# The up-projections' blocks reordered once in memory, and a folding piece fetched by one load in place of 16

## The chip, the cores and the metric

The kernel runs on one core of a Trainium2 chip. The metric is the device time of one execution in microseconds (us); lower is better. The time before is 2107.13 us, the median of 3 runs (2104.47 to 2111.49). The core's engines are TensorE (PE in the profile; PEld is its weight load), VectorE (DVE), ScalarE (ACT), GpSimd (POOL) and SyncE (SP). SP does no arithmetic here: it issues DMAs, one after the other, and waits for what each needs before it issues it. A DMA's data is then moved by 16 DMA engines that all queues share.

## What is computed

Two layers, all in float32. Both normalise their input, add an attention branch and a feed-forward branch to it, and pass the sum on:

```
xn = layernorm(x);  x = x + attn0(xn) + ffn0(xn)
xn = layernorm(x);  x = x + attn1(xn) + ffn1(xn)
```

- `attn0`: a test-time-training scan. For 4 sequences of 512 tokens and 32 heads of width 16, in 32 steps of 16 tokens, a small weight matrix per head is updated by a gradient, and read by the queries.
- `ffn0`: `silu(gate) * up`, then `down`; width 512 to 1408 and back.
- `attn1`: latent attention, 16 heads of width 128. Keys and values come from a latent of 128 columns, queries from one of 384. The rotary part of a head (64 columns) is a further product with `W_QR` or `W_KR`:

```
c_kv = xn @ W_DKV + b_DKV;  k = c_kv @ W_UK;  v = c_kv @ W_UV
c_q  = xn @ W_DQ  + b_DQ;   q = c_q  @ W_UQ
q[..., :64] = rope(q @ W_QR);  k[..., :64] = rope(k @ W_KR)
probs = softmax(q k^T / sqrt(128));  out = (probs @ v) @ W_O + b_O
```

- `ffn1`: four experts, each a gated feed-forward of width 512.

`W_UK` is [128, 2048], `W_UQ` [384, 2048] and `W_UV` [128, 2048]; the 2048 columns are 16 heads of 128.

## The kernel before

The kernel is one function, `trunk_kernel`. Its order on each engine is set by a scheduler that builds the program: it moves independent instructions past each other, by its own estimate of when they are ready. Only instructions wrapped in `pin` or `fetch` (`keep_in_program_order`) keep the written order on their engine. The many small DMAs on SP are not pinned.

**Layer 0** (the trace's first 930 us or so). Tokens go in 8 chunks of 256 columns. A generator `between(ch)` (line 636) lists the work of a chunk beside the scan: 11 gate-up blocks `gate_up(ch, i)` (line 448), the normalisation and projections of the next chunk, and two `down` passes (line 464). Each piece yields its cost in us; the scan's loop (line 761) calls `fill(us)` in its gaps, which takes pieces from this list until their costs cover the gap. A gate-up block loads two weight tiles of 256 KB, `wg` and `wu` (line 454, two buffers of each), and makes 8 products of them (helper `mm`, line 100). A `down` pass loads 11 tiles `wd` of 256 KB (line 470, four buffers). A load can be issued as soon as TensorE is done with the buffer's last content. All of them, the rows of the scan's keys and values (`rows`, `kv`) and its results (`z`, line 437) go through SP's queue.

**The experts** (about 930 to 1175 us): `hidden` and `returned`, lines 940 to 974. The weights of the attention's first head group are folded beside them.

**Attention of layer 1** (about 1175 to 2107 us). The 16 heads go in 4 groups of 4. A unit is one head of one batch: 4 groups x 4 batches x 4 heads = 64 units, in the loop of line 1259. In unit i TensorE makes keys and queries (`pk`, line 1053; `pq`, line 1061) and scores (`sc`, line 1071), VectorE and ScalarE make the probabilities of unit i-1, VectorE turns them in blocks of 32 x 32 (`tt`, line 1100), and `turn` (line 1125) puts the blocks in their places by 16 DMAs of 64 KB on SP (line 1131). The context product of unit i-3 (`pc`, line 1139) reads them. Output products of a finished batch (`p`, `px`, line 1182) are spread over the units that follow. Once per batch the latents of the next one are loaded (`cq`, line 819, three DMAs).

**Folding** (`fold`, line 827). `W_QR` and `W_KR` are multiplied into the up-projections, and `W_UV` into `W_O`, one head group at a time, so that no unit pays for it. A group has five pieces: `W_UK`, the three row blocks of `W_UQ`, and `W_UV`, each 128 rows x 4 heads x 128 columns. The products need a piece transposed. VectorE transposes within blocks of 32 x 32 (`wt`, line 852), so the load must put the 4 x 4 blocks of each head into their transposed places: line 862 does this with 16 DMAs for each piece, one for each quarter of the columns (`dq`) and each head, of 16 KB in runs of 128 bytes. `raw` has two buffers in the attention stage. A step of the generator loads piece i, transposes piece i-2 and multiplies piece i-3 (`pw`, line 847). The loop advances it once in three of four units, from the second batch of the group before. The first 64 columns of each head go to `uk` and `uq` by a DMA each (line 832), and rows of `W_O` to `ow` (line 838, on GpSimd's queue in the attention stage).

Of the kernel before, what the change touches and what calls it, by code (L numbers as in the profile page):

```python
# [12 lines left out]
F32 = mybir.dt.float32  # L13
# [5 lines left out]
P = 128  # L19
# [25 lines left out]
H, D, KVC, QC, RD = 16, 128, 128, 384, 64  # L45
# [3 lines left out]
HPG = H // NHG  # L49
# [6 lines left out]
def trunk_kernel(ctx: ExitStack, tc: tile.TileContext, a: dict, out: bass.AP):  # L56
    nc = tc.nc
# [12 lines left out]
    dram = ctx.enter_context(tc.tile_pool(name="dram", bufs=1, space=bass.MemoryType.DRAM))  # L70
    yd = dram.tile([B, L, HS], F32, tag="yd", name="yd")
    xe_d = dram.tile([2 * NCHUNK, P, NC, E, 32], F32, tag="xe_d", name="xe_d")
    lat_d = dram.tile([1 + QC // P, P, B, NCHUNK, CT], F32, tag="lat_d", name="lat_d")
    bo = const.tile([P, HS], F32, tag="bo", name="bo")
    eps_ttt = const.tile([P, 1], F32, tag="eps_ttt", name="eps_ttt")
    nc.vector.memset(eps_ttt, TTT_EPS)

# [11 lines left out]
    with ExitStack() as px:  # L89
# [7 lines left out]
        quarters = [slice(32 * q, 32 * q + 32) for q in range(4)]  # L97

        def mm(out, lhsT, rhs, start=True, stop=True):
            nc.tensor.matmul(out, lhsT=lhsT, rhs=rhs, start=start, stop=stop, skip_group_check=True)  # L100

        def psum():
            return ps_pj.tile([P, 512], F32, tag="pj", name="pj")
# [48 lines left out]
        def by_head(name):  # L152

            return a[name].rearrange("(al r) (be bp h d) -> al r be bp h d", al=4, be=4, bp=2, h=2)[:, 0, :, 0]
# [4 lines left out]
        for name in ("gamma", "beta"):  # L159
            nc.scalar.dma_start(  # L160
                out=row[name].rearrange("o (be al x) -> o be al x", be=NC, al=4),
                in_=by_head(name).rearrange("al be h d -> be al (h d)").unsqueeze(0),
# [26 lines left out]
        for h in range(2):  # L189
            r = slice(4 * h, 4 * h + 4)  # L190
            nc.gpsimd.dma_start(
                out=sel8[r], in_=a["bones"].rearrange("(be h r) p -> h be r p", be=4, h=2)[h, :, 0]
# [4 lines left out]
        for al in range(4):  # L197
            for h in range(2):
                src = a["W1"].rearrange("p (be bp h d) -> p be bp h d", be=4, bp=2, h=2)
# [248 lines left out]
        def gate_up(ch, i):  # L448
            if i == 0:
                hid[ch] = wk.tile([P, NI, CW], F32, tag="hid", name=f"hid_{ch}", bufs=1)  # L450
            pf = ps_ff.tile([P, 2, CW], F32, tag="pf", name=f"pf_{ch}_{i}")
            for j, nm in enumerate(("wg", "wu")):
                w = wk.tile([P, NC, P], F32, tag=nm, name=f"{nm}_{ch}_{i}")
                nc.sync.dma_start(out=w, in_=a[nm][i])
                for c in range(NC):
                    mm(pf[:, j, :], w[:, c, :], xTs[ch][:, c, :], c == 0, c == NC - 1)
            sg = wk.tile([P, CW], F32, tag="sg", name=f"sg_{ch}_{i}")
            nc.scalar.activation(sg, pf[:, 0, :], AF.Silu, scale=gs[:, i : i + 1])  # L458
            nc.vector.scalar_tensor_tensor(  # L459
                hid[ch][:, i, :], pf[:, 1, :], us[:, i : i + 1], sg, ALU.mult, ALU.mult  # L460
            )
            yield 3.43
# [20 lines left out]
        for j, name in enumerate(("gamma", "beta")):  # L483
            nc.gpsimd.dma_start(
                out=ch8[4 * j : 4 * j + 4], in_=by_head(name).rearrange("al be h d -> be al (h d)")
# [150 lines left out]
        def between(ch):  # L636
# [4 lines left out]
            for i in range(NI):  # L641
                yield from gate_up(ch, i)
                if ch + 1 == NCHUNK and i in (2, 5, 8):
                    latent_rows(i // 3)
                if i == NI - 3:
                    yield from take(fin, 1)
# [162 lines left out]
    quarters = [slice(32 * q, 32 * q + 32) for q in range(4)]  # L809
# [4 lines left out]
    ups = ["uk"] + [f"uq{i}" for i in range(QC // P)]  # L814
# [11 lines left out]

    def fold(w, hg, wk, psum, bufs, pin=lambda ins: ins, ahead=1, rows=nc.sync):

        c = slice(hg * HPG * D, (hg + 1) * HPG * D)
        srcs = [a["W_UK"][:, c]] + [a["W_UQ"][i * P : (i + 1) * P, c] for i in range(QC // P)]  # L830
        for nm, src in zip(ups, srcs):
            nc.sync.dma_start(out=w[nm][:, :, :RD], in_=src.rearrange("p (h d) -> p h d", h=HPG)[:, :, :RD])
        srcs.append(a["W_UV"][:, c])
        raws, turned, ows = {}, {}, {}

        def output_rows(h):
            ows[h] = wk.tile([P, HS], F32, tag="ow", name=f"ow_{hg}_{h}", bufs=2)
            rows.dma_start(out=ows[h], in_=a["W_O"][(hg * HPG + h) * D : (hg * HPG + h + 1) * D, :])

        n = len(srcs)  # L840
        for i in range(n + 1 + ahead):
            k = i - ahead - 1
            if 0 <= k < n - 1:
                wt, wr, to = turned.pop(k), wqr if k else wkr, w[ups[k]]
                pw = psum(f"pw_{hg}_{i}").rearrange("p (h d) -> p h d", h=HPG)[:, :, :RD]
                for h in range(HPG):
                    pin(nc.tensor.matmul(pw[:, h, :], lhsT=wt[:, h, :], rhs=wr, start=True, stop=True))
                pin(nc.scalar.copy(to[:, :, RD:], pw))
            if 0 <= i - ahead < n:
                t = turned[i - ahead] = wk.tile([P, HPG, P], F32, tag="wt", name=f"wt_{hg}_{i - ahead}", bufs=1)  # L850
                pin(
                    nc.vector.transpose(
                        out=t.rearrange("p h c -> p (h c)"), in_=raws.pop(i - ahead).rearrange("p h c -> p (h c)")
                    )
                )
            if i < n:

                raw = raws[i] = wk.tile([P, HPG, P], F32, tag="raw", name=f"raw_{hg}_{i}", bufs=bufs)
                view = srcs[i].rearrange("(cq r) (h dq d) -> dq r h cq d", r=32, h=HPG, dq=4)
                for dq, r in enumerate(quarters):  # L860
                    for h in range(HPG):
                        nc.sync.dma_start(  # L862
                            out=raw[r, h].rearrange("r (cq d) -> r cq d", cq=4), in_=view[dq, :, h]
                        )
            if i - n - ahead + 1 >= 0:
                output_rows(i - n - ahead + 1)
            yield
        wt = turned.pop(n - 1)
        for h in range(HPG):
            pv = psum(f"pvo_{hg}_{h}")  # L870
            pin(nc.tensor.matmul(pv, lhsT=wt[:, h, :], rhs=ows[h], start=True, stop=True))
            pin(nc.scalar.copy(w["vo"][:, h, :], pv))
            hh = hg * HPG + h
            if hh == 0:
                pin(nc.vector.tensor_scalar_mul(bo_part, ows[h], buv[:, :1]))
            else:
                pin(nc.vector.scalar_tensor_tensor(bo_part, ows[h], buv[:, hh : hh + 1], bo_part, ALU.mult, ALU.add))
            if h + 2 < HPG:
                output_rows(h + 2)
            if h == 1:  # L880
                yield
        if hg == NHG - 1:
            pb = psum("pbo")
            pin(nc.tensor.matmul(pb, lhsT=ones, rhs=bo_part, start=True, stop=True))
            pin(nc.vector.tensor_add(bo, pb, bo))

    with ExitStack() as px:
# [88 lines left out]
        for e in range(E):  # L976
            if e == 1:
                nc.sync.dma_start(out=wqr, in_=a["W_QR"])
                nc.sync.dma_start(out=wkr, in_=a["W_KR"])
                buv16 = wk.tile([H, D], F32, tag="sg", name="buv16")  # L980
                nc.sync.dma_start(out=buv16, in_=a["b_UV"].rearrange("(h d) -> h d", d=D))
                w0 = group_tiles(lat, 0)
                cqs = {(0, 0): batch_latents(0, 0)}
                first = fold(w0, 0, wk, lambda nm: psp.tile([P, 512], F32, tag="pa", name=nm), 1)
                nc.sync.dma_start(out=buk, in_=a["b_UK"])
                nc.sync.dma_start(out=buq, in_=a["b_UQ"])
                for k in range(E):
                    nc.sync.dma_start(
                        out=trig_k[RD:, :].rearrange("p (k e j) -> p k e j", k=NCHUNK, e=E)[:, :, k],
                        in_=a["trig"][:, k * P : (k + 1) * P].rearrange("p (k j) -> p k j", k=NCHUNK),  # L990
                    )
                nc.sync.dma_start(out=ckv, in_=lat_d[0].rearrange("p b k x -> p b (k x)"))
# [28 lines left out]
    with ExitStack() as px:  # L1021
# [5 lines left out]
        def pin(ins):  # L1027
            tc.keep_in_program_order(ins)
            return ins
# [229 lines left out]
        for i in range(nu + 1):  # L1259
            if i < nu:  # L1260
                hg, b, h = units[i]
# [24 lines left out]
            if i >= 3:  # L1286
                hg, b, h = units[i - 3]
# [5 lines left out]
            k = i - (nu - HPG * B)  # L1293
# [113 lines left out]
```

## Time and profile before

| | |
|---|---|
| median of 3 runs | 2107.13 us |
| the profiled execution | 2108.69 us |
| its span, first to last instruction | 2106.9 us |
| mean granted TensorE clock | 0.982 of full speed |
| TensorE busy | 2004.7 us (95%) |
| VectorE, ScalarE, GpSimd busy | 1245.9, 843.3, 585.9 us |
| DMA share of SP's queue (q1) | 43.7% of 16 engines' span |
| DMAs of line 1131 | 1008, 0.60 us to issue (median) |
| DMAs of line 862 | 320, 0.43 us to issue (median) |

Several views are used. The page gives totals, the chain of work that ended last (each stretch of the span put down to the engine and line that released what came next), and the costliest groups of instructions, each with the idle time of the engine before it and what ended that. A timeline lists instructions in order of time, with equal neighbours merged. The stretches view gives, for chosen stretches: the length, then the busy time and number of instructions of PE, PEld, DVE, ACT and POOL, then the granted clock, the DMA share and GB/s. An engine with a `q` behind its name is that engine's sequencer, which waits and issues. The list of DMA issues gives size and median time from issue to landing.

### The profile page before, as it was taken

How to read it: one execution, taken by the hardware profiler on the slowest of the kernel's cores; microseconds unless marked ns; L12 is line 12 of the kernel's file. 1: busy time of each engine (PE TensorE's matmuls, PEld its weight loads, DVE VectorE, ACT ScalarE, POOL GpSimd, SP SyncE). 2: the span in 40 equal slices, each digit the busy share in tenths (PEclk: the TensorE clock that was granted, in tenths of full speed). 3: DMA queues.
4: the chain of work that ended last, by engine and by line, in shares of the span. 5: the costliest groups of instructions: out<-in, count | busy, mean ns of one | idle time of the engine just before them, and what ended most of it. 6: DMA issues, size and time to landing. Idle time of an engine off the chain costs nothing.

```text
span 2106.9 us, 30312 instructions
## 1 busy us (share of the span) xinstructions
PE 2004.7 (95%) x10294; PEld 1222.7 (58%) x10294; DVE 1245.9 (59%) x2578; ACT 843.3 (40%) x1699; POOL 585.9 (28%) x635
## 2 busy tenths in 40 slices
PE   8999999899999997997999898999999998999998
PEld 6777676767676865634444344555555554555554
DVE  5446666474747485542112586777667775777772
ACT  2334343333334443311001464555445554555552
POOL 4333333323333332201001132223223232254320
PEclk9999999999999999998999999999999999999999
DMA  6546464645554645535721243534344334433332
GB/s 181 153 136 197 121 197 107 180 137 172 142 165 131 187 138 164 164 98 203 245 76 59 54 105 87 122 98 102 81 103 120 81 91 92 114 94 93 94 99 82
DMA packets 342213, 266.70 MB, mean 127 GB/s; under 512 B 107819, under 2 KB 265708, under 8 KB 341420
## 3 DMA queue, kind: packets, MB, share of 16 engines
q1 hardware_dynamic: 327072, 250.18, 43.7%
q0 software_dynamic: 3488, 9.27, 1.4%
q10 hardware_dynamic: 11500, 5.32, 0.9%
q8 instruction: 83, 1.36, 0.3%
q14 instruction: 70, 0.57, 0.1%
HBM read 168.94 MB, written 29.62 MB: 94 GB/s over the span
## 4 chain that ended last, share of the span: by engine, by line
PE 77%; DVE 7%; SPq 6%; DMA 5%; ACT 3%; issue 2%; POOL 0%; ACTq 0%; DVEq 0%; POOLq 0%
PE pf L100 12%; PE pj L100 12%; PE pc L1139 9%; PE sc L1071 8%; PE pq L1061 7%; PE pd L100 6%; SPq L1131 4%; PE px L1182 4%; PE epg L924 3%; PE p L1182 3%; PE epo L967 3%; PE epu L924 3%; PE pk L1053 2%; PE pz L100 2%; SPq L862 1%
## 5 line engine op out<-in xcount | busy, mean ns | idle before, releaser
L1139 PE MATMUL pc<-prT,lv 128*128 128x512 f32 x496 | 235.5, 620 | 25.0 <-DMA prT<-tt 13.2
L1076 ACT ACTIVATE prob<-sc,mx 128x512 f32<-128x512 f32 x256 | 174.3, 683 | 192.4 <-DVE mx L1073 188.4
L1071 PE MATMUL sc<-kT,qT 96*128 96x512 f32 x512 | 230.9, 593 | 0.9 <-ACT prob L1076 0.6
L1100 DVE STREAM_TRANSPOSE tt<-prob 128x512 f32<-128x512 f32 x252 | 172.8, 705 | 90.0 <-DMA prT<-tt 46.3
L1046 POOL TENSOR_TENSOR kT<-t_k,t_k 32x512 f32<-32x512 f32 x64 | 80.6, 1259 | 431.5 <-PE pq L1061 244.5
L100 PE MATMUL pf<-xT,wg 128*128 128x256 f32 x704 | 175.8, 393 | 13.7 <-DVE hid L459 7.0
L1081 ACT ACTIVATE prob<-prob,sm 128x512 f32<-128x512 f32 x256 | 176.3, 713 | 0.0
L1061 PE MATMUL pq<-cq,uq 128*128 128x512 f32 x384 | 175.6, 593 | 0.7 <-DVE t_k L1042 0.6
L1139 PEld LDWEIGHTS pc<-prT,lv 128*128 128x128 f32 x496 | 98.3, 200 | 128.7 <-issue 125.3
L1073 DVE TENSOR_REDUCE mx<-sc 128x1 f32<-128x512 f32 x256 | 168.1, 677 | 6.7 <-PE sc L1071 4.4
L100 PE MATMUL pf<-xT,wu 128*128 128x256 f32 x704 | 169.4, 384 | 0.0
L1071 PEld LDWEIGHTS sc<-kT,qT 96*128 96x128 f32 x512 | 97.0, 190 | 124.7 <-issue 119.8
L100 PE MATMUL pd<-wd,hid 128*128 128x512 f32 x352 | 165.8, 601 | 1.5 <-DMA wd<-in_wd 1.2
L100 PEld LDWEIGHTS pf<-xT,wg 128*128 128x128 f32 x704 | 133.5, 194 | 40.7 <-DVE hid L459 9.8
L100 PEld LDWEIGHTS pf<-xT,wu 128*128 128x128 f32 x704 | 136.5, 194 | 19.3 <-DMA wu<-in_wu 0.2
L1061 PEld LDWEIGHTS pq<-cq,uq 128*128 128x128 f32 x384 | 72.7, 190 | 93.5 <-issue 82.0
L459 DVE SCALAR_TENSOR_TENSOR hid<-pf,us,sg 128x256 f32<-128x256 f32 x88 | 42.1, 480 | 141.2 <-ACT sg L458 140.3
L404 POOL TENSOR_SCALAR gh<-grad,m 128x256 f32<-128x256 f32 x64 | 63.3, 999 | 173.7 <-DVE grad L373 159.1
L297 POOL TENSOR_SCALAR sk<-k,m 128x256 f32<-128x256 f32 x64 | 59.9, 947 | 178.8 <-PE pz L100 165.6
L100 PEld LDWEIGHTS pd<-wd,hid 128*128 128x128 f32 x352 | 63.7, 190 | 60.8 <-issue 46.4
L1046 POOL TENSOR_TENSOR qT<-t_q,t_q 32x512 f32<-32x512 f32 x64 | 80.7, 1260 | 58.1 <-DVE t_q L1042 58.0
L458 ACT ACTIVATE sg<-pf,gs 128x256 f32<-128x256 f32 x88 | 41.4, 473 | 128.1 <-PE pf L100 127.6
(273 smaller groups left out, 3380.9 us busy)
## 6 DMA issues: line engine op xcount, KB each, us to landing
prT<-tt SPq DMA_DIRECT2D x1008, 64.0 KB, 2.0
wd<-in_wd SPq DMA_DIRECT2D x176, 256.0 KB, 3.0
wg<-in_wg SPq DMA_DIRECT2D x88, 256.0 KB, 2.9
wu<-in_wu SPq DMA_DIRECT2D x88, 256.0 KB, 3.2
cq<-lat_d SPq DMA_DIRECT2D x48, 256.0 KB, 3.9
rows<-rows SPq DMA_DIRECT2D x128, 66.0 KB, 2.2
kv<-rows SPq DMA_DIRECT2D x32, 264.0 KB, 4.5
gu<-in_gu SPq DMA_DIRECT2D x3, 2048.0 KB, 7.9
```

The costliest lines, as they stand in the source:

```text
L100: nc.tensor.matmul(out, lhsT=lhsT, rhs=rhs, start=start, stop=stop, skip_group_check=True)
L924: nc.tensor.matmul(ps, lhsT=w[:, c, col : col + P], rhs=xe[:, :, c, e, :], start=(c == 0), stop=(c == NC - 1))
L1046: nc.gpsimd.tensor_sub(t[RD:mid, :], t1[RD:mid, :], t2[RD:mid, :])
L1061: nc.tensor.matmul(pq, lhsT=w[f"uq{i}"][:, h, :], rhs=cqs[hg, b][:, i, :], start=(i == 0), stop=(i == nq - 1))
L1071: pin(nc.tensor.matmul(ps, lhsT=qT[:KQ, i * P : (i + 1) * P], rhs=kT[:KQ, :], start=True, stop=True))
L1073: pin(nc.vector.tensor_reduce(mx, ps, AX.X, ALU.max, negate=True))
L1076: pin(nc.scalar.activation(pr, ps, AF.Exp, bias=mx, scale=1.0, accum_out=sm))
L1081: pin(nc.scalar.mul(pr, pr, sm))
L1100: nc.vector.transpose(out=tt[:, :, :, i, :], in_=pr.rearrange("p (kb e j) -> p kb e j", e=2, j=K))
L1131: nc.sync.dma_start(out=prT[32 * kq : 32 * kq + 32, :, qb, :], in_=src[32 * qb : 32 * qb + 32, :, kq, :])
L1139: pin(nc.tensor.matmul(pc, lhsT=lv[:, b, k, :], rhs=prT[:, k, :], start=(k == 0), stop=(k == E - 1)))
L1182: nc.tensor.matmul(ps[:, q, :], lhsT=a[:, k, q * P : (q + 1) * P], rhs=w[:, k, :], start=start and k == 0 and q == 0, stop=k == 1, skip_gr ...
```

## The change

A buffer `blocks_d` in memory holds all five row blocks of the up-projections with their 32 x 32 blocks already in transposed places. A generator `reordered` fills it by 80 DMAs from memory to memory on SP's queue, 16 for each row block: each takes one 32 x 32 block of all 16 heads, 64 KB in 512 runs of 128 bytes. Gate-up blocks 0 to 9 of each of the 8 chunks of layer 0 issue one copy each. In `fold` one load of 256 KB, in runs of 2 KB, takes the place of the 16 loads of a piece. The sources of `uk` and `uq` are the same as before, written as a cut of the whole matrix. The number of 128-byte runs is 80 x 512 = 40960 in the copies, as it was in the loads before (320 x 128).

```diff
+    blocks_d = dram.tile([QC // P + 2, P, H, P], F32, tag="blocks_d", name="blocks_d")
+    up_srcs = [a["W_UK"]] + [a["W_UQ"][i * P : (i + 1) * P] for i in range(QC // P)] + [a["W_UV"]]
+
+    def reordered():
+
+        for k, src in enumerate(up_srcs):
+            view = src.rearrange("(cq r) (h dq d) -> cq dq r h d", r=32, dq=4, d=32)
+            for cq in range(4):
+                for dq in range(4):
+                    nc.sync.dma_start(
+                        out=blocks_d[k, 32 * dq : 32 * dq + 32, :, 32 * cq : 32 * cq + 32], in_=view[cq, dq]
+                    )
+                    yield
+
+    copies = reordered()
...
                 for c in range(NC):
                     mm(pf[:, j, :], w[:, c, :], xTs[ch][:, c, :], c == 0, c == NC - 1)
+            if i < 10:
+                next(copies, None)
             sg = wk.tile([P, CW], F32, tag="sg", name=f"sg_{ch}_{i}")
...
-        c = slice(hg * HPG * D, (hg + 1) * HPG * D)
-        srcs = [a["W_UK"][:, c]] + [a["W_UQ"][i * P : (i + 1) * P, c] for i in range(QC // P)]
-        for nm, src in zip(ups, srcs):
-            nc.sync.dma_start(out=w[nm][:, :, :RD], in_=src.rearrange("p (h d) -> p h d", h=HPG)[:, :, :RD])
-        srcs.append(a["W_UV"][:, c])
+        heads = slice(hg * HPG, (hg + 1) * HPG)
+        for nm, src in zip(ups, up_srcs):
+            nc.sync.dma_start(out=w[nm][:, :, :RD], in_=src.rearrange("p (h d) -> p h d", h=H)[:, heads, :RD])
...
             if i < n:
-
                 raw = raws[i] = wk.tile([P, HPG, P], F32, tag="raw", name=f"raw_{hg}_{i}", bufs=bufs)
-                view = srcs[i].rearrange("(cq r) (h dq d) -> dq r h cq d", r=32, h=HPG, dq=4)
-                for dq, r in enumerate(quarters):
-                    for h in range(HPG):
-                        nc.sync.dma_start(
-                            out=raw[r, h].rearrange("r (cq d) -> r cq d", cq=4), in_=view[dq, :, h]
-                        )
+                nc.sync.dma_start(out=raw, in_=blocks_d[i][:, heads, :])
```

In the built order of the changed kernel, chunk 0 differs most. The load of `wo` (1 MB, line 497 of before) stands on SP between `wg` and `wu` of block 8 instead of behind block 1, and the first load of `kv` behind `wu` of block 4 instead of behind block 3. On TensorE the products that make constants from `wo`, and the transposes and first projections of chunk 1, come after gate-up blocks 2 to 10 instead of ahead of them. Elsewhere TensorE's order differs by single neighbours. Most copies stand between weight loads; in the `down` passes two or three often stand together. In the attention stage each of the single loads stands where the 16 loads of its piece stood, or up to one unit's turn from there.

More of the change, by code (lines that the diff above doesn't have):

```diff
@@ L838, in output_rows @@
             rows.dma_start(out=ows[h], in_=a["W_O"][(hg * HPG + h) * D : (hg * HPG + h + 1) * D, :])
-        n = len(srcs)
+        n = len(up_srcs)
         for i in range(n + 1 + ahead):
```

## The prediction

> **What bounds the kernel now.** I read the profiled execution: a span of 2106.9 us in a run of 2108.69 us, so 1.8 us lie outside it. The page comes first.
>
> ```profile
> PE 77%; DVE 7%; SPq 6%; DMA 5%; ACT 3%; issue 2%; POOL 0%; ACTq 0%; DVEq 0%; POOLq 0%
> L1139 PE MATMUL pc<-prT,lv 128*128 128x512 f32 x496 | 235.5, 620 | 25.0 <-DMA prT<-tt 13.2
> raw<-in_W_UQ SPq DMA_DIRECT2D x192, 16.0 KB, 1.8
> ```
>
> TensorE carries the chain, but the queue of SyncE (SPq) has 6% of it, and TensorE idles 25.0 us before the context products of line 1139, mostly for transfers. So I looked for stretches where SP sets the pace. I cut the attention stage into units, one head of one batch each, from the first `pk` product (line 1053) of one to that of the next. A plain unit takes 13.76 us. These do not: units 9 and 10 (15.72 and 22.84 us), 25 and 26 (21.37 and 20.01), 41 and 42 (20.20 and 21.27). All hold fold work for the next head group. The stretches view sets 25 and 26 beside two plain units; the first number is the length, the second TensorE's busy time:
>
> ```profile
> 1497.36:1518.72 21.36, 16.52 (x49) 8.95 (x48) 11.31 (x21) 7.87 (x16) 2.52 (x2) 0.92 0.33 67
> 1518.72:1538.73 20.01, 16.59 (x50) 8.99 (x50) 10.47 (x19) 7.65 (x16) 2.52 (x2) 0.91 0.51 128
> 1608.87:1622.63 13.76, 13.76 (x41) 7.61 (x40) 10.61 (x20) 7.28 (x15) 3.61 (x4) 1.00 0.67 169
> 1622.63:1636.39 13.76, 13.76 (x42) 7.61 (x41) 9.88 (x19) 7.30 (x15) 2.52 (x2) 1.00 0.34 81
> ```
>
> A plain unit is all TensorE. In the long ones it idles 3.4 to 4.8 us, the granted clock falls to 0.91-0.92, and DMA is busy for a third to a half of the time. What is short is SP's time to issue, as the timeline of SP says (start, length, what):
>
> ```profile
> 1482.42 8.98 SPq L1131 DMA_DIRECT2D prT<-tt  x14
> 1491.49 9.12 SPq L862 DMA_DIRECT2D raw<-in_W_UQ  x16
> 1500.72 10.26 SPq L1131 DMA_DIRECT2D prT<-tt  x16
> 1511.09 7.87 SPq L862 DMA_DIRECT2D raw<-in_W_UQ  x16
> 1519.05 1.32 SPq L819 DMA_DIRECT2D cq<-lat_d  x3
> 1520.49 20.01 SPq L1131 DMA_DIRECT2D prT<-tt  x31
> ```
>
> SP issues without rest for 58 us. One unit's turn (16 DMAs, line 1131) costs 10.3 us of it, a folding piece (16 DMAs, line 862) 7.9: 18.2 us, where TensorE needs 14.7. TensorE's timeline shows who pays:
>
> ```profile
> 1512.68 5.37 PE L1139 MATMUL pc<-prT,lv 128*128 128x512 f32 x8 [4.84 <-DMA raw<-in_W_UQ]
> 1532.69 5.37 PE L1139 MATMUL pc<-prT,lv 128*128 128x512 f32 x8 [3.42 <-DMA prT<-tt]
> ```
>
> The products wait for turned blocks issued behind the pieces, and then run 5.37 us instead of the plain unit's 3.43.
>
> **Removed: 15 SP deficits in the attention stage.** Five pieces in each of four groups go from 16 loads to one. Group 0 folds under the experts and part of group 1 before the first turn; TensorE is busy 80.00 of 80 us and 88.84 of 90 in 1020-1190, so nothing is to be had there. In the attention stage a piece now costs one issue, about 0.44 us (a `cq` load above: 1.32/3), and saves 7.4. A folding unit then asks SP for 10.3 + 0.4 = 10.7 us, 12 to 13 with a batch's `cq` loads, under TensorE's 12.95 to 14.68, so the deficit is gone. What would the long units take? A plain one (13.76) plus eight `pw` products: 12.95 - 12.03 = 0.92, from otherwise equal units 39 and 35. So 14.68. Excess: 15.72 + 22.84 - 29.36 = 9.2; 21.37 + 20.01 - 29.36 = 12.0; 20.20 + 21.27 - 29.36 = 12.1; unit 29 (14.16 for 13.76) 0.4. **Sum -33.7 us.** What is late next is TensorE itself. If SP were half of the cause, 17 would go; these are the ends I keep. Unit 3 (17.68 us) keeps its excess: SP waits there 4.7 us for VectorE's `tt`, not for a piece.
>
> The new load waits for the copies, which end in the last chunk, over 100 us before the first fold, and for a `raw` buffer that VectorE's `wt` frees, as before. Behind it on SP stand turns whose `tt` VectorE makes after that `wt`, so it holds nothing that could go. One 256 KB load landed in 2.9 us (`wg`), and a piece is used two fold steps on. W_O's rows on POOL's queue stay.
>
> **Added: 80 copies in layer 0.** Each gate-up block 0 to 9 of eight chunks issues one: 64 KB in 512 runs of 128 B, memory to memory, on SP's queue between the weight loads. No memory-to-memory DMA is in this trace. Issue: like `z` (512 runs as well), 0.51 us median; SP waits 255.7 us for line 454's buffers and 146.2 for line 470's, which hides 80 x 0.51 = 41. Transfer: in the packet records 128 B loads (`raw`) took 13 ns each, at 32 per engine 0.43 us a copy; `z`'s stores of 256 B moved at 154 GB/s (stretch 371.80 to 376.90), 0.85 us for 512. I take 0.85, since a copy also stores short runs to memory. The far end is 2.9 us, `z`'s whole time from issue to landing. At 0.85 the copies add 68 us of transfer to 870 us whose DMA share is 0.54, so it becomes 0.62:
>
> ```profile
> 30.00:900.00 870.00, 831.60 (x6933) 606.46 (x6936) 511.77 (x1224) 324.65 (x616) 269.66 (x346) 0.98 0.54 154
> wd<-in_wd SPq DMA_DIRECT2D x176, 256.0 KB, 3.0
> wg<-in_wg SPq DMA_DIRECT2D x88, 256.0 KB, 2.9
> z<-zch SPq DMA_DIRECT2D x32, 128.0 KB, 2.9
> ```
>
> A copy hurts only if it makes a weight load late. For the 226 loads of `wg`, `wu` and `wd` with a known landing I took the time from landing to first product: under 0.85 us for 9%, 1.7 us for 19%, 2.9 us for 38%. The mean shortfall of a load pushed back by d is 0.015 us at d = 0.43, 0.046 at 0.85, 0.167 at 1.7, 0.53 at 2.9. A copy delays at most the two loads behind it, so the cost is 160 x 0.046 = **+7.4 us** (2.4 at 0.43, 27 at 1.7, 85 at 2.9).
>
> The Trainium skill (DMA: Bandwidth & Descriptors, Specifications) asks for at least 512 B per transfer for line rate and says that below it the engine reads, modifies and writes. The trace leans that way: `z`'s 256 B stores ran at 154 GB/s. Were each run handled twice by that rule, the copies would cost the 27 of the first rival.
>
> **Moved.** The built order also shifts in chunk 0: the 1 MB load of `wo` leaves the start of SP's queue for a place between `wg` 8 and `wu` 8, and the first `kv` load goes behind `wu` 4. TensorE fills the place with gate-up blocks 2 to 10, some 31 us that cover the later gradient. `wu` 8 lands about 2.6 us later (`ckv`'s 1 MB landed in 5.5 us, a 256 KB load in 2.9), and a late load falls short by 0.53 at 2.9: **+1 us**, rounded up. The new order may also give back up to the 4.83 us that TensorE idles in 30-150. The rest of TensorE's order differs by a few swapped neighbours; I put that at nothing, since the work before a swapped product is as long as after it, and within 5 either way.
>
> **Sum:** -33.7 + 7.4 + 1.0 = -25.3, so 2108.69 becomes 2083.4. The median of the runs shown is 1.56 under the profiled run: 2081.8, say **2082 us**.
>
> **Rivals.** (1) Each copy takes two passes, 1.7 us: -33.7 + 27 + 1 gives 2101. For it: short runs both read and stored in memory. Against: packet times that grow with size, 13 ns at 128 B, 25 for `z`. (2) **Slower:** the copies run at 2.9 us each on all engines, 232 us of transfer, the share in layer 0 rises to 0.81, and weights come late throughout: -33.7 + 85 + 1 gives 2159. It decides from 1.9 us per copy on, where the shortfall reaches 0.204 us a load (32.7/160). For it: no row excludes it. Against: 2.9 us is mostly latency, since four `z` stores together ran at 0.85 each. (3) SP was only half of the stall, VectorE's transposes or the landing the rest: -17 + 8.4 gives 2098.5. Against: the windows show VectorE busy half the time. (4) The change does not do what it says: the merged load arrives late or the new order costs in layer 0 what attention gains; 2105.
>
> **How the numbers follow.** Forecast 0.68, rivals 0.11, 0.10, 0.07 and 0.04. A measurement of this kernel tells about 0.3%, or 6.3 us, from no change: 2100.8 to 2113.5. Faster takes the forecast, rival 3 and half of rival 1: 0.80; within: the rest of 1 and rival 4, 0.09; slower: 2, with 0.01 from rivals 1 and 4, 0.11. The range goes from -33.7 with copies free and 5 us from the order (2069) up to rival 1 (2101); the forecast's own spread is 2070 to 2092.
>
> **What would show it.** Right: units 9, 10, 25, 26, 41 and 42 at 14.7 us and clock 1.00, no long SP run without rest there, `pc`'s mean back near 593 ns, and 30-900 us grown by about 8 us. Wrong: units still at 20 us, or TensorE waits on `wg`, `wu`, `wd` in layer 0 that grow by more than 30 us from today's 6.4, with copies landing far above 3 us.

## The result, and the profile after

The changed kernel takes **2083.71 us** (median of 4 runs, 2079.54 to 2087.11) where the kernel before takes 2105.89 on the same chip (4 runs, 2104.47 to 2111.49): a ratio of 0.9889, 95% interval 0.9863 to 0.9915. A repeat on another chip gave 2087.42 against 2106.49, ratio 0.9910 (0.9897 to 0.9924). The profiled run took 2079.54 us, with a span of 2077.8.

First the chain of work, the `pc` group (the second number after the bar is the mean in ns, the last part the idle time before it), and two rows of the list of DMA issues, after the change:

```profile
PE 83%; DVE 6%; DMA 5%; ACT 2%; SPq 1%; issue 1%; POOL 0%; ACTq 0%; DVEq 0%; POOLq 0%
L1150 PE MATMUL pc<-prT,lv 128*128 128x512 f32 x496 | 224.7, 596 | 3.9 <-DMA prT<-tt 3.9
raw<-blocks_d SPq DMA_DIRECT2D x20, 256.0 KB, 3.5
blocks_d<-in_W_UQ SPq DMA_DIRECT2D x48, 64.0 KB, 2.9
```

SP's part of the chain went from 6% to 1%, TensorE's idle time before `pc` from 25.0 to 3.9 us. The stretches of units 25 and 26, and two plain ones (length; busy time of PE, PEld, DVE, ACT, POOL; then granted clock, DMA share, GB/s):

```profile
1494.94:1509.53 14.59, 14.59 (x49) 8.43 (x48) 10.51 (x20) 7.87 (x16) 2.52 (x2) 1.00 0.54 131
1509.53:1524.18 14.65, 14.65 (x50) 8.49 (x50) 10.71 (x20) 7.66 (x16) 2.52 (x2) 1.00 0.38 90
1537.10:1550.92 13.82, 13.82 (x43) 7.66 (x43) 10.71 (x21) 7.07 (x15) 2.52 (x2) 1.00 0.45 116
1550.92:1564.68 13.76, 13.76 (x42) 7.60 (x41) 9.90 (x19) 7.30 (x15) 2.52 (x2) 1.00 0.37 94
```

TensorE is busy for the whole of each folding unit, at full clock. SP's timeline of the same stretch:

```profile
1467.48 10.25 SPq L1142 DMA_DIRECT2D prT<-tt  x16
1477.83 0.53 SPq L875 DMA_DIRECT2D raw<-blocks_d  x1
1481.27 10.72 SPq L1142 DMA_DIRECT2D prT<-tt  x16
1492.09 0.54 SPq L875 DMA_DIRECT2D raw<-blocks_d  x1
1492.72 1.34 SPq L838 DMA_DIRECT2D cq<-lat_d  x3
```

A piece costs SP 0.53 us where it cost 7.9 to 9.1, and SP rests between a turn's last DMA and the next turn (1478.4 to 1481.3). From the first `pk` product to the end of the span the kernel before takes 932.2 us (from 1174.7), the changed one 896.9 (from 1181.0): 35.4 gained.

Ahead of it 6.3 us are lost. Three rows of the list of TensorE's waits in 0-930 us (total, times, longest), those on `gh` and on weights, first of before, then of after:

```profile
PE pf L100 <- DMA wg<-in_wg: 5.2, 2, 4.1
PE pso L100 <- POOL gh L404: 3.3, 3, 1.7
PE pd L100 <- DMA wd<-in_wd: 1.2, 2, 0.6
```

```profile
PE pso L117 <- POOL gh L421: 12.0, 6, 5.9
PE pf L117 <- DMA wg<-in_wg: 4.2, 2, 3.9
PE pd L117 <- DMA wd<-in_wd: 0.9, 2, 0.5
```

Waits on weights, where I had put the cost of the copies, fell. What grew most is the wait on GpSimd's `gh`, in which 5.9 us are one wait. The longest row of both lists, the state product's wait on `g_bd`, went from 12.3 to 13.6 us, and all rows together from 47.0 to 54.6. TensorE's timeline shows it, in scan step 4 (start, length, what, and in brackets the idle time before):

```profile
168.10 0.63 PE L117 MATMUL pso<-wq_bd,wh 128*32 128x64 f32 x32
168.66 3.70 PE L117 MATMUL pd<-wd,hid 128*128 128x512 f32 x8
178.28 0.43 PE L117 MATMUL pso<-a_bd,gh 128*32 128x68 f32 x2 [5.93 <-POOL gh L421]
178.51 0.42 PE L117 MATMUL wacc<-g_bd,km 128*32 128x64 f32 x2
178.86 3.78 PE L117 MATMUL pf<-xT,wu 128*128 128x256 f32 x8
```

The same place before the change, where the `wu` half of block 6 stands ahead of the `pz` product (175.35) instead:

```profile
173.62 1.89 PE L100 MATMUL pf<-xT,wu 128*128 128x256 f32 x8
175.35 0.60 PE L100 MATMUL pz<-gsum,bones 128*128 128x256 f32 x2
175.87 1.08 PE L100 MATMUL pz<-wq_bd,sk 128*32 128x128 f32 x32
176.77 0.63 PE L100 MATMUL pso<-wq_bd,wh 128*32 128x64 f32 x32
177.33 3.70 PE L100 MATMUL pd<-wd,hid 128*128 128x512 f32 x8
180.87 1.89 PE L100 MATMUL pf<-xT,wg 128*128 128x256 f32 x8
```

In the new order one output product and one state product of step 4 stand ahead of that `wu` half and of blocks 7 to 10. TensorE ran its products in the built order, so while the output product waits for `gh`, gate-up work waits behind it; that this work was ready shows in e3 below, where the same `wu` products run at 172.44. Then the eight `wu` products take 3.78 us, not 1.89: the clock row of the stretch after the wait reads 0.50.

```profile
178.28:182.44 4.16, 4.16 (x13) 3.27 (x14) 0.00 (x0) 0.00 (x0) 0.00 (x0) 0.50 0.02 4
```

The Trainium skill (TensorE: Matmul & The Clock Gate, Part 1: The HAM clock gate) says that TensorE falls to half rate after about 3.4 us of idling and needs as long to recover; 5.93 us of idling and the doubled time agree. I read from VectorE's timeline where each scan step's gradient (`grad`) ends. From step 4 to step 5: 30.4 us before, 40.8 after.

### The profile page after: what moved, and what is told of

Same layout as the page of the kernel before. It is cut to its first block, busy times and chain, and to the rows that moved or that the text cites. A ratio compares the mean times of both kernels' runs of the same rounds, so it can differ in the third digit from the quotient of the medians.

```text
span 2077.8 us, 30073 instructions
## 1 busy us (share of the span) xinstructions
PE 1989.2 (96%) x10294; PEld 1216.1 (59%) x10294; DVE 1246.7 (60%) x2578; ACT 838.3 (40%) x1695; POOL 588.4 (28%) x635
## 3 DMA queue, kind: packets, MB, share of 16 engines
q1 hardware_dynamic: 326112, 255.41, 45.3%
## 4 chain that ended last, share of the span: by engine, by line
PE 83%; DVE 6%; DMA 5%; ACT 2%; SPq 1%; issue 1%; POOL 0%; ACTq 0%; DVEq 0%; POOLq 0%
PE pf L117 13%; PE pj L117 13%; PE pc L1150 10%; PE sc L1082 10%; PE pq L1072 8%; PE pd L117 6%; PE px L1193 5%; PE p L1193 4%; PE epo L978 3%; PE pk L1064 3%; PE epu L935 2%; PE pz L117 2%; PE epg L935 2%; DMA lat_d<-lat 2%; PE pso L117 1%
## 5 line engine op out<-in xcount | busy, mean ns | idle before, releaser
L1150 PE MATMUL pc<-prT,lv 128*128 128x512 f32 x496 | 224.7, 596 | 3.9 <-DMA prT<-tt 3.9
L117 PE MATMUL pf<-xT,wg 128*128 128x256 f32 x704 | 176.4, 393 | 12.3 <-DVE hid L478 6.8
```

The lines of the kernel that those rows point to most:

```text
L1150: pin(nc.tensor.matmul(pc, lhsT=lv[:, b, k, :], rhs=prT[:, k, :], start=(k == 0), stop=(k == E - 1)))
```

## The experiments

Theory O: the merged loads give all of the gain; the copies cost nothing to move, but the scheduler orders the rest of layer 0 differently because of them, and that costs. Rival T: the copies' transfers cost, by late weights or otherwise. "Steps 1 to 31" is the time between those gradients' ends in the profiled run; steps count from 0.

| kernel | median us | ratio to before, 95% interval | step 4 to 5 | steps 1 to 31 |
|---|---|---|---|---|
| before | | | 30.4 | 798.4 |
| changed | 2083.71 | 0.9889 (0.9863 to 0.9915) | 40.8 | 809.4 |
| the same again | 2087.42 | 0.9910 (0.9897 to 0.9924) | 40.6 | 812.3 |
| e1 loads alone | 2072.52 | 0.9844 (0.9825 to 0.9862) | 30.4 | 797.5 |
| e2 copies alone | 2116.31 | 1.0053 (1.0038 to 1.0068) | 41.0 | 812.2 |
| e3 order mended | 2081.29 | 0.9886 (0.9868 to 0.9904) | 35.0 | 805.2 |
| e5 copies of 12 heads | 2075.47 | 0.9854 (0.9835 to 0.9872) | 30.4 | 798.8 |
| e6 thin copies | 2075.05 | 0.9850 (0.9835 to 0.9864) | 30.4 | 802.7 |
| e8 copies in long runs | 2074.61 | 0.9846 (0.9831 to 0.9860) | 30.4 | 804.4 |
| e7 copies on ScalarE's queue | 2075.06 | 0.9850 (0.9825 to 0.9875) | 32.5 | 800.6 |
| e4 copies twice | 2085.12 | 0.9900 (0.9883 to 0.9916) | 33.0 | 812.9 |
| e9 copies by scan step | 2080.94 | 0.9872 (0.9856 to 0.9888) | 31.4 | 802.9 |
| e10 copies from chunk 1 on | 2089.63 | 0.9923 (0.9910 to 0.9935) | 40.4 | 810.5 |
| e11 the same, mended | 2085.88 | 0.9907 (0.9888 to 0.9925) | 36.6 | 808.1 |

Before had medians of 2105.97 (e1 to e3, e5), 2105.93 (e4, e6 to e8), 2106.49 (e9, e10, the repeat) and 2104.39 (e11).

**e1, the loads alone.** No copies; each piece is one load straight from the source (its blocks stay unturned).

```diff
-            if i < 10:
-                next(copies, None)
...
-                nc.sync.dma_start(out=raw, in_=blocks_d[i][:, heads, :])
+                nc.sync.dma_start(out=raw, in_=up_srcs[i].rearrange("p (h d) -> p h d", h=H)[:, heads, :])
```

> Each piece by one load of 256 KB straight from the up-projection, in its own order (the 32 x 32 blocks are not put in transposed places, so the folded weights are wrong by this); no copies in layer 0. Every engine but SP has the order of before. My theory: the whole gain is SP's issue time in the attention stage, 35.4 us between the traces (932.2 to 896.9 us from the first pk product to the end), and layer 0 is as before: about 2070.5 us, with the first pk product at 1174.7 us. Rival 1, that half of the stall was VectorE or landing: units 9, 10, 25, 26, 41 and 42 near 17 us, 2088. Rival 2, that part of the 35 us came with the new order of layer 0 and not with the loads: 2076 or more.

Measured 2072.52, 33.4 under before and 2 over the expected 2070.5. TensorE's order is that of before, and units 25 and 26 take 14.59 and 14.65 us. The merged loads alone give the predicted gain.

**e2, the copies alone.** The kernel before, with `blocks_d` filled but not read.

```diff
+            if i < 10:
+                next(copies, None)
```

> The 80 copies are made, but the pieces are still fetched by 16 loads from the up-projections. TensorE has the order of the changed kernel. My theory: layer 0 costs what the traces show, 6.3 us up to the first pk product, and attention is as before: 2112 us, units 25 and 26 at 20 to 21 us. Rival, that copies and loads help each other (the merged loads also shorten layer 0): the first pk product not at 1181 but at 1190 us or later, 2120. Rival, the copies are free and the 6.3 us are between one execution and another: 2106.

Measured 2116.31: 10.3 more than before, where 6 were expected; between the two profiled runs it is 6.6 (the first unit starts at 1181.3 instead of 1174.7). Units 25 and 26 take 20.58 and 20.02 us, before 21.37 and 20.01. TensorE's order is that of the changed kernel, and so is its wait on `gh`, 12.0 us. The two parts add up: -33.4 + 10.3 = -23.1, against -22.2 for the whole. Whether the 10.3 is transfer or order, e2 does not say.

**e3, the order mended.** In the changed kernel, step 4's state and output products and step 5's first ones are kept behind block 6 of chunk 1.

```diff
+            with ExitStack() as behind:
+                if n == 4:
+                    behind.enter_context(tc.issue_after(gated[1, 6].ins))
+                update(n, g, pre)
+                fill(gaps[1])
+                emit_out(n, po, gh)
```

> The changed kernel with TensorE's order mended in one place: the products of scan step 4's update and output, and of step 5's start, are kept behind the second half of gate-up block 6 of chunk 1. In the changed kernel one product for pso and one for wacc stand ahead of that half, and TensorE stood still for 5.93 us for gh there and then ran eight products in 3.78 us in place of 1.89. My theory: the layer 0 loss is that swap, not the copies' transfers: 7.8 us less than the changed kernel, 2076 us. Rival, weight loads made late by copies: the stall moves to a wait for wu, same time as the changed kernel, 2084.

The wait on `gh` fell from 12.0 to 4.6 us, and step 5's gradient ends at 211.4 instead of 216.9. But of these 5.5 us only 2.2 are left at the first unit (1178.8 against 1181.0), and the median is 2081.29, not the expected 2076: a smaller gain, inside the intervals of the changed kernel. One reason is in the trace. The `wu` products of block 6 now run at once, but two blocks later TensorE waits for VectorE's `hid`, where the changed kernel does not:

```profile
172.44 1.89 PE L117 MATMUL pf<-xT,wu 128*128 128x256 f32 x8
180.65 1.99 PE L117 MATMUL pf<-xT,wg 128*128 128x256 f32 x8 [2.87 <-DVE hid L478]
```

The repair also changes some 50 rows of TensorE's order elsewhere, so it is not clean.

**e5, copies of 12 heads.** The first head group folds by 16 loads as before; the copies (384 runs of 128 bytes each) are written in the code at the third expert.

```diff
+            if e == 2:
+                for _ in copies:
+                    pass
```

> The copies leave layer 0: all 80 are issued at the start of expert 2 and cover heads 4 to 15 alone (384 runs in place of 512 each); the first group's pieces come by 16 loads as before, the others by one. TensorE's order in layer 0 is nearly that of before. My theory: SP has room under the experts (TensorE is busy 80.00 of 80 us in 1020-1100 us, DMA share 0.42, and 0.18 in 1100-1190), 80 copies take 80 x 0.5 = 40 us to issue there, and nothing waits for them: the gain of the loads alone, 2071 us. Rival, the copies push back the expert weights or the first group's pieces on the one queue: TensorE waits on gu or dn, or units 0 to 3 late, by 5 to 20 us: 2076 to 2091.

The trace overturns the placing that the expectation took for granted: the scheduler hoisted the copies into layer 0, where they are issued on SP's queue between 89 and 421 us (in the changed kernel between 14 and 457). That makes it the best test of T: three quarters of the same short runs, on the same queue in the same chunks, but TensorE's order differs from that of before in 33 rows only, that of the changed kernel in more than 80. Steps 1 to 31 take 798.8 us, before 798.4. The first unit starts 3.7 us later than before (1178.4), but as much is there at the end of step 0, at 76.0 us, ahead of any copy. The time is 2075.47, 4.5 over the expected 2071 and 3 over e1. The waits of 0-930 us:

```profile
PE pf L117 <- DMA wg<-in_wg: 6.5, 4, 4.2
PE pso L117 <- POOL gh L421: 3.4, 3, 1.7
PE pd L117 <- DMA wd<-in_wd: 1.0, 2, 0.7
```

T falls here for these copies: TensorE waits for weights 7.5 us in all, 6.4 before and 7.6 in e1.

**e6, thin copies, and e8, long runs.** In e6 each copy moves one head in 16, and pieces are loaded from the sources; in e8 it moves its 64 KB in 32 runs of 2 KB.

```diff
-                        out=blocks_d[k, 32 * dq : 32 * dq + 32, :, 32 * cq : 32 * cq + 32], in_=view[cq, dq]
+                        out=blocks_d[k, 32 * dq : 32 * dq + 32, :1, 32 * cq : 32 * cq + 32], in_=view[cq, dq][:, :1]
```

```diff
-            view = src.rearrange("(cq r) (h dq d) -> cq dq r h d", r=32, dq=4, d=32)
+            view = src.rearrange("(dq r) (h d) -> dq r h d", r=32, h=H)
...
-                        out=blocks_d[k, 32 * dq : 32 * dq + 32, :, 32 * cq : 32 * cq + 32], in_=view[cq, dq]
+                        out=blocks_d[k, 32 * dq : 32 * dq + 32, 4 * cq : 4 * cq + 4], in_=view[dq, :, 4 * cq : 4 * cq + 4]
```

> Computes something else in the folds: the 80 copies move one head in 16 (32 runs of 128 bytes instead of 512), and the single loads read the sources directly, with blocks not turned. TensorE's order is close to that of the mended kernel: the up half of block 6 in chunk 1 is ahead of scan step 4's last products. Theory (the copies' transfers cost nothing, the order alone does): the wait on POOL's gh stays near 3.4 us, the first attention product comes where the mended kernel has it, 1179, or earlier by what is left of order, and the time is 2079 to 2082, like the mended kernel's 2081.3. Rival (the bytes of the copies delay something in layer 0 that the waits do not name): the bytes are gone, so the time is that of the loads alone, 2072.5, and the first attention product comes near 1172.

> Computes something else in the folds: each of the 80 copies moves its 64 KB in 32 runs of 2 KB instead of 512 of 128 bytes, so the blocks are not turned. The order of TensorE has no up half behind the scan in chunk 1. Theory (transfers cost nothing): 2079 to 2082, like the mended kernel. Rival 1 (the short runs cost): 2072 to 2075. Rival 2 (bytes cost, whatever their runs): like the mended kernel with full copies, 2081, while the thin copies come out near 2073. Landing of a copy: near 2.9 us if it is latency, under 2.5 us if the short runs make it.

Measured 2075.05 and 2074.61: my expectations by the theory, 2079 to 2082, missed, since I had taken e3's time for the price of an order without the swap. Full bytes in long runs cost no more than a sixteenth of them. Taken alone, the pair would fit "short runs cost"; e5 speaks against that, and so does e7's time. Long runs do not land sooner either. The changed kernel's three rows of copies landed in 2.9, 3.0 and 2.8 us; those in e8's list of DMA issues:

```profile
blocks_d<-in_W_UQ SPq DMA_DIRECT2D x48, 64.0 KB, 2.9
blocks_d<-in_W_UK SPq DMA_DIRECT2D x16, 64.0 KB, 3.8
blocks_d<-in_W_UV SPq DMA_DIRECT2D x16, 64.0 KB, 3.2
```

What the short runs do take is time of the 16 DMA engines. SP's queue in e1, which has no copies, in the changed kernel and in e8 (packets, MB, share of 16 engines' span):

```profile
q1 hardware_dynamic: 283872, 250.16, 43.8%
q1 hardware_dynamic: 326112, 255.41, 45.3%
q1 hardware_dynamic: 287712, 255.41, 44.4%
```

45.3% of 2077.8 us less 43.8% of 2070.7 is 34 us, or 0.43 us for each of 80 copies; in e8 (44.4% of 2073.6) it is 0.17.

**e7, the copies on ScalarE's queue.**

```diff
-                    nc.sync.dma_start(
+                    nc.scalar.dma_start(
                         out=blocks_d[k, 32 * dq : 32 * dq + 32, :, 32 * cq : 32 * cq + 32], in_=view[cq, dq]
```

> The 80 copies are issued by ScalarE instead of SP, between the activations of layer 0, and TensorE's order is close to that of the kernel before (no up half of block 6 behind the scan). Theory (neither the transfers nor the short runs cost, the order does): first attention product at 1174 to 1177, time 2074 to 2077. Rival 1 (transfers cost): 2081 to 2084, as after the change. Rival 2 (issue on ScalarE costs: 80 x 0.5 us = 40 us on an engine that makes sg, g_bd and wq_bd for the scan): waits of TensorE on ACT in layer 0 grow from some 5 us by 10 or more, 2085 to 2110.

Measured 2075.06, as the theory said; the first unit starts at 1172.3, before at 1174.7. All 80 copies, with all their short runs, are issued by 177 us, more densely than in any other kernel. TensorE's order is 48 rows from before. Here weights do come later:

```profile
PE pf L117 <- DMA wg<-in_wg: 11.6, 7, 4.3
PE pf L117 <- DVE hid L478: 5.7, 2, 3.9
PE pso L117 <- POOL gh L421: 3.3, 3, 1.7
```

TensorE waits 13.0 us for weights (7.6 in e1), and 4.7 of these 5.4 us more lie ahead of 177 us, where the copies are. All its waits in 0-930 us come to 47.0 us, the same as before (45.3 in e1). So e7 shows no net loss, but it does not clear transfers that stand this close together: other waits got shorter, and which part of that is order was not separated.

**e4, every copy twice**, the second into a buffer that nothing reads.

```diff
+                    nc.sync.dma_start(
+                        out=again_d[k, 32 * dq : 32 * dq + 32, :, 32 * cq : 32 * cq + 32], in_=view[cq, dq]
+                    )
```

> Every copy is made twice, the second time into a buffer that nothing reads: 160 copies, 136 us of transfer at 0.85 us each, and 80 us of issue on SP. TensorE's order differs in many places from the changed kernel, and the up half of block 6 in chunk 1 is not behind the scan. Theory (transfers are hidden, order decides): 2076 to 2082; weights come no later, waits on wg and wd stay under 8 us. Rival (late weight loads, as predicted: 7.4 us for 80 copies): twice 7.4, 2088 to 2092, with waits on wg, wu and wd grown by about as much.

Measured 2085.12, between the two expectations: no more than the changed kernel, with waits on `wg` of 6.0 us. But its order differs from every other kernel's in hundreds of rows, so it decides little.

**e9 and e10, the copies from other places, and the changed kernel again.** In e9 the scan's loop issues three copies a step; in e10 the gate-up blocks of chunks 1 to 7 issue them. In both, as in the changed kernel, the built order moves the copies forward: they are issued from 18.8 to 520.5 us in e9 and from 82.7 to 525.1 in e10. e9's order has no swap in chunk 1; e10's keeps it.

```diff
+            for _ in range(3):
+                next(copies, None)
             if n + 1 < NM:
```

```diff
-            if i < 10:
+            if ch > 0:
                 next(copies, None)
+                if (ch, i) in ((7, 2), (7, 5), (7, 8)):
+                    next(copies, None)
```

> The same 80 copies of 512 runs of 128 bytes, on SP's queue and during layer 0, but issued by the scan's loop, three in a step, instead of by the gate-up blocks. In the built order the up half of block 6 in chunk 1 is ahead of scan step 4's last products again, and no pair of state and output products is torn apart before step 13. Theory (the order costs, the copies do not): 2073 to 2078, step 4 to 5 near 30 us, wait on gh near 3.4 us. Rival (copies of this form on this queue cost, in any order): 2082 to 2086.

> The same 80 copies on SP's queue, issued by the gate-up blocks of chunks 1 to 7 instead of 0 to 7. TensorE's order is 26 rows from that of the changed kernel and keeps the up half of block 6 in chunk 1 behind scan step 4's last products; chunk 0 is as before the change. Theory (that order costs): step 4 to 5 near 40 us, wait on gh near 12 us, 2081 to 2086. Rival (the order is worth little, the copies beside chunk 0 cost): 2073 to 2078.

> The changed kernel itself, beside the other two on the same chip, so that differences of 5 us can be told: 2080 to 2087 by either theory.

e10, with the swap: 2089.63, above what I had expected. e9, without it: 2080.94, 3 us above the theory's range and 1 us below the rival's. The repeat of the changed kernel took 2087.42, just above the 2080 to 2087 that I had expected. e9 and e10 copy the same bytes in the same runs. e10's timeline in step 4, then e9's:

```profile
174.09 3.70 PE L117 MATMUL pd<-wd,hid 128*128 128x512 f32 x8
183.71 0.43 PE L117 MATMUL pso<-a_bd,gh 128*32 128x68 f32 x2 [5.92 <-POOL gh L421]
183.94 0.42 PE L117 MATMUL wacc<-g_bd,km 128*32 128x64 f32 x2
184.29 3.77 PE L117 MATMUL pf<-xT,wu 128*128 128x256 f32 x8
```

```profile
173.81 3.70 PE L117 MATMUL pd<-wd,hid 128*128 128x512 f32 x8
177.35 1.89 PE L117 MATMUL pf<-xT,wg 128*128 128x256 f32 x8
179.08 1.89 PE L117 MATMUL pf<-xT,wu 128*128 128x256 f32 x8
```

The `pd` products start 0.3 us apart; step 5 then ends at 222.0 in e10 and at 212.6 in e9, and 8.3 us of that are left at the first unit (1190.2 against 1181.9), 8.7 in the medians. e9's excess over e8, 6.3 us, stands almost whole at step 1 (107.9 against 102.3), so it arises in chunk 0, where the two orders differ; that the order makes it is not shown. From step 1 to 31 the short runs of e9 take 802.9 us, the thin ones of e6 802.7.

**e11, e10 mended**, by the edit of e3.

> The kernel with copies in chunks 1 to 7, where the swapped order stood alone beside an unchanged chunk 0 and cost most (2089.6 us, ratio to before 0.9923), with that order mended: step 4's state update and output and step 5's first products are kept behind both halves of block 6 of chunk 1. Theory (the swap costs some 8 to 10 us, of which step 4 to 5 shows 10): step 4 to 5 back from 40.4 to about 31 us, ratio 0.987 to 0.990, some 2080 to 2084. Rival (only a local shift, given back by the end of layer 0): ratio 0.991 or more, 2087 and above.

Step 5 ends at 212.8 instead of 222.0, but 5.4 of these 9.2 us are there at the end of step 4 already, ahead of the mended place. From step 4 to 5 it takes 36.6 us instead of 40.4, not the expected 31, with the same 2.87 us of waiting for `hid` as in e3. The first unit starts 4.0 us earlier (1186.2), and the ratio, 0.9907 against 0.9923, lies between the two expectations, with intervals that overlap. As in e3, the repair pushes other products aside: steps 10 to 15 give some back, and so do the experts.

## Why the prediction came out, step by step

- **"Sum -33.7 us" in the attention stage: right, by its mechanism.** 33.4 by e1's medians, 35.4 between the two profiled runs; from the first unit on, e1 gains 33.8 and the repeat 33.7. The six long units take 14.59 or 14.65 us, predicted 14.68. Unit 3 kept its excess (17.17).
- **"160 x 0.046 = +7.4 us": failed, in the size of a transfer and in what it does.** A copy took 0.43 us of the DMA engines' time (see e8), the figure from packet times that the prediction set aside for 0.85; with it, its sum would have been -30.3. The 2.9 us from issue to landing, my far end, are not transfer. And in the changed kernel weights came no later than before: waits on `wg` and `wd` fell by 1.3 us, and the mean shortfall of a load pushed back by 0.85 us fell from 0.046 to 0.029. e5 puts the transfers' cost at 0.4 us in steps 1 to 31; e7, where copies stand closest, shows later weights but no net loss. The model let each copy push back the two loads behind it; the runs do not show how far that happens. The copies also end at 457 us, not in the last chunk, which does no harm.
- **"+1 us" for `wu` 8 in chunk 0: not seen.** No wait of TensorE's products on `wu` is in the trace. Chunk 0 even gained: step 4 ends 8.7 us earlier than before; e1, whose order is that of before, shows 3.0 of that as well, so about 5.7 can be due to the order.
- **"The rest of TensorE's order differs by a few swapped neighbours; I put that at nothing ... within 5 either way": the step that failed.** One swap goes with 10.4 us from step 4 to 5 (40.8 against 30.4) and with 8.7 in the medians of e10 and e9; undone in its place, it gave back 5.5 us at step 5 in e3, and 3.8 from step 4 to 5 in e11. My reason, that the work before a swapped product is as long as after it, leaves out that a product waits for another engine: put ahead of ready work, it made all of it wait for 5.93 us, and the granted clock was 0.50 after that.
- **The sum: right by two errors that cancel, which is luck.** -25.3 predicted, -22.2 measured: 8.4 us were charged to late weights and none to order. What was lost is 6.3 us up to the first unit in the profiled run, and 11.2 by the medians of e1 and the changed kernel; the traces put most of it to waits that came with the order, and none to weights. The repeat (-19.1) lies within the range too.
- **The rivals.** The copies at 1.7 or 2.9 us each fall with the measured 0.43, and a stall that SP only half explains falls with e1. The Trainium skill (DMA: Bandwidth & Descriptors, Specifications) asks for at least 512 B per transfer for line rate. The trace agrees as far as the DMA engines' time goes: a copy took 0.43 us of all 16 in runs of 128 B, and 0.17 in e8's runs of 2 KB. In e5's time the short runs show no price. "The new order costs in layer 0 what attention gains" was the rival with the true mechanism, at half its price or less: e10, the worst order, costs 17 us over e1, attention gains 33.

**Open.** How the rest of the order's cost is shared. Besides the swap, the changed kernel loses 3.4 us between the ends of steps 13 and 15, of which 1.9 come back by step 17, and from the first expert's products to the first unit it takes 179.7 us and its repeat 181.6, before 177.9, although TensorE's order is the same there. Kernels with the same order differ by 3 us from the first step on (before and e1), so single steps of that size are not settled. Neither repair of the swap showed a gain beyond its interval, so its price lies somewhere between the 2.2 us that e3 kept at the first unit and the 8.7 of the pair e9 and e10, which differ in other rows as well. What copies cost that stand as close as in e7 is open too.

The best kernels that compute the whole are e5 and e7: ratios 0.9854 and 0.9850, about 8 us under the changed kernel's 2083.71; their intervals lie below that of its repeat, and overlap that of its first measurement.

## What to carry to other kernels

Where a queue's issue time is longer than the unit it feeds, the deficit can be read unit by unit; here merging the DMAs gave back just that. Added DMAs whose transfer is hidden are not yet free: if a scheduler builds the order, compare the built orders on the in-order engine, and look for products that wait for another engine and now stand ahead of ready ones. Test such a cost with kernels that move the same bytes in another order, before blaming the bytes.

## What the runs showed of the hardware

- Memory-to-memory copies of 64 KB in 512 runs of 128 B cost 0.51 us to issue, landed in 2.9 us (the rows of `W_UQ`), and took 0.43 us of the 16 DMA engines; in 32 runs of 2 KB (e8) they landed in 2.9 us as well and took 0.17. Eighty of them within 177 us (e7) made TensorE wait 5.4 us longer for weights than in e1, with no net loss of time.
- After 5.9 us of idling, TensorE ran at a granted clock of 0.50 for 4.2 us: eight products took 3.78 us instead of 1.89, in the changed kernel and in e10. There the wait cost 1.9 us more than its length.
